# Splitting five block products of the last two projections once more, with their weight sums made ahead on VectorE

## The chip, the cores and the metric

The kernel runs on one core of a Trainium2 chip. The metric is the device time of one execution in microseconds (us), as the median of several runs. Engines are named as the profile names them: PE is TensorE's matmul, PEld its weight load, DVE is VectorE, ACT is ScalarE, POOL is GpSimd, SP is SyncE, which issues most of the transfers here. Each engine works through its own instructions in program order.

## The reference

A cross-attention block in float32: 4 batches of 512 rows, width 512, 16 heads, 512 context rows. The part that the change touches is the MLP at the end.

```python
x = layer_norm(hidden_states, ln1_w, ln1_b)
...
attn = jax.nn.softmax(scores, axis=-1)
out = jnp.einsum('bhqk,bhkd->bhqd', attn, v)
...
out = out @ cproj_w + cproj_b
hidden = out + residual
residual = hidden
y = layer_norm(hidden, ln2_w, ln2_b)
y = jax.nn.gelu(y @ fc_w + fc_b, approximate=True)
y = y @ proj_w + proj_b
return residual + y
```

`fc_w` is 512 x 2048 and `proj_w` 2048 x 512. Everything is float32.

## The kernel before

**Two stages.** The first is attention for all batches, with the MLP of batch 0 and half of that of batch 1 worked in between. The order of instructions is written out by hand. The second stage, `last_mlps` (L590), holds the rest: the second half of batch 1 (`SPLIT` is 1), then batch 2, then batch 3, one after the other. For each batch it runs fc for pairs of 128-wide chunks of the inner dimension (four pairs for batch 1, eight for batches 2 and 3), then proj.

**Seven products instead of eight.** Both matrix products use the Strassen-Winograd scheme: a product of 2 x 2 blocks is made from seven block products, of sums of blocks that other engines prepare. For a left matrix A and a right matrix B the sums are s1 to s4 and t1 to t4, and the products are q1 to q7. `a_sums` (L457) makes s1 to s4 with one add and three subtractions, `b_sums` (L463) t1 to t4. Some sums overwrite a block of their input (`b12` becomes t3, `a21` becomes s3).

- fc: `fc_seven` (L483) does seven products for a pair of chunks, each of two matmuls with 256 columns. Its right sums are `y_sums` (L472), made once per batch from the transposed normed rows `yT` into `ys`; its left sums are those of the weights, `sum_wa` (L580), for pair c+1 while pair c is multiplied. Raw weights and sums have two places each in `gt` (`wa`, `ws`). The two gelus of ACT (L513) leave the result in `ga`.
- proj: `project` (L613). The left matrix is `ga`, its blocks g11 to g22, its sums `gs` from `g_sums` (L603) for two pairs at a time; the right one is the proj weights in `pbt`, their sums in `ptt`, from `p_sums` (L584) for two pairs at a time. Each of the seven products, q1, q2, q3, q6, q7, q5, q4 in this order, is 16 matmuls of 128 x 128 weights and 256 columns for batches 2 and 3 (two row halves t, eight pairs c), and 8 for batch 1. A float32 matmul is two instructions in the profile.

**What stands around the products in `project`.** After q1, `sums()` loads the residual rows of the next batch (`load_hid`, L397), whose bias row GpSimd adds (L357, four adds of 128 x 512); in batch 2 it also made the weight sums `p_sums` for four pairs. After q2, `turns()` transposes the next batch's normed rows on PE (`ln_turn`, L154). Each product's result is joined into the residual rows: VectorE reads PSUM (`join(nc.vector, ...)`, and the adds into `u2p` and `u3p`), GpSimd adds what lies in SBUF (`p1p`, `u2p`, `u3p`). After q5, `middle()` makes the next batch's `y_sums` and `sum_wa(0)` on VectorE; the next batch's fc starts with two products that need neither and a third that needs both. PSUM has four banks of `acc` and four of `half`.

**Batch 3's layernorm.** `cproj` (L382) adds the attention output to rows that lie in the first half of `pbt`, and SP stores them to `xa`. In batch 1's proj, `load_xn` brings them back; during batch 2's fc, VectorE makes their statistics (`stat2`, L406: one bn_stats and one bn_aggr per 128 rows), GpSimd the reciprocal root (`ln_rs`, L131), and VectorE the normed rows (`norm2`, `ln_norm`, L144). `BY_ACT` (L42) lists the norms that ScalarE applies.

**The proj weights of the first four pairs** are loaded during batch 2's fc (L677 to L679), into the part of `pbt` where queries and keys, and then batch 3's rows, lay before.

Of the kernel before, what the change touches and what calls it, by code (L numbers as in the profile page):

```python
# [12 lines left out]
F32 = mybir.dt.float32  # L13
# [7 lines left out]
P = 128  # L21
# [3 lines left out]
NT = L // P  # L25
# [13 lines left out]
IN_XE = (25, 27, 29, 31)  # L39

AT = {u: (u - 5) // 2 for u in (5, 7, 9, 11, 13, 15, 17, 19, 53, 55, 57, 59, 61, 63)}
BY_ACT = ((1, 1), (1, 2))  # L42
MW = 8
WARM = 9
PW = 2 * NT * HG * HD
# [7 lines left out]
def xattn_block(ctx: ExitStack, tc: tile.TileContext, x, encT, mask, q_w, k_w, v_w, c_w, fc_w, p_w, vecs, rows, out):  # L53
# [77 lines left out]
    def ln_rs(key):  # L131

        ve = small.tile([P, NT], F32, tag="ve", name=f"ve{key[0]}_{key[1]}")
        nc.gpsimd.tensor_scalar(ve, S["mv", key][:, :, 1], EPS, 1.0, ALU.add, ALU.mult)
        rs = small.tile([P, NT], F32, tag="rs", name=f"rs{key[0]}_{key[1]}")
        nc.gpsimd.tensor_tensor(rs, ve, nhalf, ALU.pow)
        S["rs", key] = rs
        if key in BY_ACT:
            nm = small.tile([P, NT], F32, tag="nm", name=f"nm{key[0]}_{key[1]}")
            nc.gpsimd.tensor_tensor(nm, S["mv", key][:, :, 0], rs, ALU.mult)  # L140
            nc.gpsimd.tensor_scalar(nm, nm, -1.0, 0.0, ALU.mult, ALU.add)
            S["nm", key] = nm
# [11 lines left out]
    def ln_turn(key, d, xn, dst):  # L154

        w, bi = (LN1W, LN1B) if key[0] == 1 else (LN2W, LN2B)
        tp = acc_tile(f"tp{key[0]}_{key[1]}_{d}")
        for t in range(NT):
            nc.tensor.transpose(tp[:, ts(t, P)], xn[t][:, ts(d, P)], ident)
        wd, bd = vec[:, w + d : w + d + 1], vec[:, bi + d : bi + d + 1]  # L160
        if d in (1, 2) and key not in BY_ACT:
            nc.vector.tensor_scalar(dst[:, d, :], tp, wd, bd, ALU.mult, ALU.add)
        else:
            nc.scalar.activation(dst[:, d, :], tp, AF.Identity, bias=bd, scale=wd)
# [241 lines left out]
    def stat2(b, t):  # L406
        ln_stat((2, b), t, S["h", b, t])
# [46 lines left out]
    def add(engine, o, x0, x1):  # L454
        engine.tensor_tensor(o, x0, x1, ALU.add)  # L455
# [24 lines left out]
    def acc_half(name):  # L480
        return acc_tile(name).rearrange("p (i l) -> p i l", i=2)
# [94 lines left out]
    def load_wa(c):  # L576
        for i in range(2):
            nc.sync.dma_start(out=wa[c % 2][:, i], in_=fc_w[:, 2 * c + i, :, :])
# [5 lines left out]
    def p_sums(c):  # L584
# [2 lines left out]
        b11, b12, b21, b22 = (pb[:, c, k, j * HL : (j + 1) * HL] for k in range(2) for j in range(2))  # L587
        b_sums(b11, b12, b21, b22, pt[:, 0, c], pt[:, 1, c], b12, pt[:, 2, c])

    def last_mlps():  # L590
        last, = pools(ctx, last=1)
        ps_last = ctx.enter_context(tc.tile_pool(name="ps_last", bufs=4, space=PSUM))
        ga = last.tile([P, NP, 2, L], F32, tag="ga", name="ga")
        gs = last.tile([P, 3, NP, HL], F32, tag="gs", name="gs")
        hl = last.tile([P, NT, D], F32, tag="hl", name="hl")
        for t in range(NT):
            S["hid", SPLIT + 1, t] = hl[:, t]
        p1p, u2p, u3p = (last.tile([P, 2, HL], F32, tag=n, name=n) for n in ("p1p", "u2p", "u3p"))

        def half_tile(name):  # L600
            return ps_last.tile([P, 2, HL], F32, tag="half", name=name)

        def g_sums(c):  # L603
            c = slice(c, c + 2)
            a11, a12, a21, a22 = (ga[:, c, k, j * HL : (j + 1) * HL] for j in range(2) for k in range(2))
            a_sums(a11, a12, a21, a22, gs[:, 0, c], gs[:, 1, c], a21, gs[:, 2, c])

        def fc_pair(b, c, sums):
            sums()
            fc_seven(b, c, ga[:, c], [wa[c % 2][:, i] for i in range(2)],  # L610
                     [ws[c % 2][:, i] for i in range(4)], half_tile)

        def project(b, pairs, sums, turns, middle):  # L613
            g11, g12, g21, g22 = (ga[:, :, k, j * HL : (j + 1) * HL] for j in range(2) for k in range(2))
            b11, b12, b21, b22 = (pb[:, :, k, j * HL : (j + 1) * HL] for k in range(2) for j in range(2))
            t1, t2, t3, t4 = pt[:, 0], pt[:, 1], b12, pt[:, 2]
            s1, s2, s3, s4 = gs[:, 0], gs[:, 1], g21, gs[:, 2]

            def product(o, a, w, ts_=range(2)):
                for t in ts_:  # L620
                    for c in pairs:
                        nc.tensor.matmul(  # L622
                            o[:, t], a[:, c, ts(t, P)], w[:, c], start=(c == pairs[0]), stop=(c == pairs[-1])
                        )

            def hid(i, j, t):
                return S["hid", b, 2 * i + t][:, j * HL : (j + 1) * HL]

            def join(engine, i, j, src):
                for t in range(2):  # L630
                    add(engine, hid(i, j, t), src[:, t], hid(i, j, t))

            def store(i, j):
                for t in range(2):
                    nc.sync.dma_start(out=out[b, ts(2 * i + t, P), j * HL : (j + 1) * HL], in_=hid(i, j, t))

            q1, q2 = (acc_half(f"{n}p_{b}") for n in ("q1", "q2"))
            product(q1, g11, b11)
            nc.scalar.copy(p1p, q1)
            sums()  # L640
            product(q2, g12, b21)
            turns()
            q3 = half_tile(f"q3p_{b}")
            product(q3, s4, b22)
            join(nc.vector, 0, 0, q2)
            join(nc.gpsimd, 0, 0, p1p)
            store(0, 0)
            q6 = acc_half(f"q6p_{b}")
            product(q6, s2, t2)
            add(nc.vector, u2p, q6, p1p)  # L650
            join(nc.vector, 0, 1, q3)
            q7 = half_tile(f"q7p_{b}")
            product(q7, s3, t3)
            add(nc.vector, u3p, q7, u2p)
            for i, j, src in ((0, 1, u2p), (1, 0, u3p), (1, 1, u3p)):
                join(nc.gpsimd, i, j, src)
            q5 = half_tile(f"q5p_{b}")
            product(q5, s1, t1)
            join(nc.vector, 0, 1, q5)
            join(nc.vector, 1, 1, q5)  # L660
            store(0, 1)
            store(1, 1)
            middle()
            q4 = half_tile(f"q4p_{b}"), acc_half(f"q4p_{b}")
            for t in range(2):
                product(q4[t], g22, t4, (t,))
                add(nc.vector, hid(1, 0, t), q4[t][:, t], hid(1, 0, t))
                nc.sync.dma_start(out=out[b, ts(2 + t, P), :HL], in_=hid(1, 0, t))

        y_sums(SPLIT)  # L670

        half = FIRST * FQ // 2
        for b, pairs, new in (
            (SPLIT, range(half, NP), ()), (SPLIT + 1, range(NP), range(half)), (SPLIT + 2, range(NP), ())
        ):
            for c in pairs:
                if c in new:  # L677
                    for i in range(2):
                        nc.sync.dma_start(out=pb[:, c, i, :], in_=p_w[ts(2 * c + i, P), :])  # L679
                fc_pair(b, c, lambda: sum_wa(c + 1) if c + 1 < NP else None)  # L680
                if c + 2 < NP:
                    load_wa(c + 2)
                elif b + 1 < B:
                    load_wa(c + 2 - NP)
                if c % 2 == 0 and c != pairs[0]:
                    g_sums(c - 2)

                if b == B - 2:
                    for t in {0: (0,), 1: (1, 2), 3: (3,)}.get(c, ()):
                        stat2(b + 1, t)  # L690
                    if c == 3:
                        ln_rs((2, b + 1))
                    for t in {4: (0,), 5: (1, 2), 7: (3,)}.get(c, ()):
                        norm2(b + 1, t)
            g_sums(NP - 2)

            def sums(b=b, new=new):
                for c in new[::2]:
                    p_sums(c)
                if b + 1 < B:  # L700
                    load_hid(b + 1, range(NT))

            def turns(b=b):
                if b + 1 < B:
                    run(turns2(b + 1))
                if b == SPLIT:
                    load_xn(B - 1)

            def middle(b=b):
                if b + 1 < B:  # L710
                    y_sums(b + 1)
                    sum_wa(0)

            project(b, pairs, sums, turns, middle)
# [17 lines left out]
    def C(b):  # L732
        return [(CHAIN, lambda t=t: cproj(b, t)) for t in range(NT)]
# [190 lines left out]
    run(mlp)  # L924
    load_wa(first_c + 1)
    sum_wa(first_c)
    c = C(B - 1)
    run(c[:2])
    p_sums(first_c + 2)
    run(c[2:])  # L930
    att.close()
    last_mlps()

# [43 lines left out]
```

## Time and profile before

| | us |
|---|---|
| median of three runs | 802.96 (802.51 to 803.77) |
| the profiled execution | 801.93 |
| its span, first to last instruction | 800.2 |

The granted TensorE clock of the profiled execution is 0.998. Busy time by stretch of `last_mlps` (us):

| stretch | length | PE | DVE | ACT | POOL |
|---|---|---|---|---|---|
| batch 1 fc, 549.6 to 574.3 | 24.70 | 24.25 | 19.20 | 5.14 | 0.00 |
| batch 1 proj, 574.3 to 601.3 | 27.00 | 26.76 | 11.78 | 3.48 | 11.24 |
| batch 2 fc, 601.3 to 649.9 | 48.60 | 48.59 | 43.91 | 11.50 | 1.37 |
| batch 2 proj, 649.9 to 700.2 | 50.30 | 50.30 | 22.85 | 3.48 | 11.48 |
| batch 3 fc, 700.2 to 748.6 | 48.40 | 48.40 | 37.23 | 11.49 | 0.00 |
| batch 3 proj, 748.6 to 797.4 | 48.80 | 48.34 | 8.43 | 1.92 | 5.59 |

A line of the timeline gives the start in us from the span's start, the length in us, the engine, the line of the kernel, the operation, the tile written and those read, the shapes and how many were merged; in square brackets is how long the engine had been idle and what ended that. A line of the chain gives the start, the length and what ran. Matmuls overlap in the pipeline, so a single one's listed length is longer than its step to the next.

### The profile page before, as it was taken

Reading aid. Unit: us, or ns where it says so; the run is one execution under the profiler, and the core shown is the slowest. Engines: PE = TensorE matmul, PEld = TensorE weight load, DVE = VectorE, ACT = ScalarE, POOL = GpSimd, SP = SyncE. Lnnn points to the kernel's source line nnn. Section 1 sums busy time; section 2 is a strip of 40 time slices with the busy share of each in tenths; the row PEclk is TensorE's granted clock in tenths of the full one; section 3 lists DMA queues with packets and bytes.
Section 4 is the critical chain, followed back from the end, with each engine's and each line's share of the span. In section 5 each row is a group of like instructions: output and inputs, shape, how many; then the busy total and the mean of one; then the engine's idle time right before and its main releaser. Section 6 shows DMA issues by size and latency. Waiting matters only on the chain.

```text
span 800.2 us, 12085 instructions
## 1 busy us (share of the span) xinstructions
PE 785.3 (98%) x4178; PEld 499.4 (62%) x4178; DVE 573.8 (72%) x1179; ACT 339.5 (42%) x745; POOL 123.9 (15%) x146
## 2 busy tenths in 40 slices
PE   9999999989999999999999999999999999999998
PEld 6545455456655645556553433446888888888887
DVE  3789998888888857779878988546738983368511
ACT  2567765547763636456554479500201220022100
POOL 1210030055121141001220100020040020200011
PEclk9999999999999999999999999999999999999999
DMA  8889999847897777787777799882325330033001
GB/s 325 289 230 241 235 237 244 231 115 182 209 240 196 211 210 192 179 198 199 181 173 213 205 261 246 202 254 93 117 84 172 118 106 14 27 86 86 1 14 40
DMA packets 60957, 137.15 MB, mean 171 GB/s; under 512 B 12464, under 2 KB 15664, under 8 KB 60768
## 3 DMA queue, kind: packets, MB, share of 16 engines
q1 hardware_dynamic: 59472, 132.43, 61.3%
q0 software_dynamic: 896, 2.82, 1.1%
q10 hardware_dynamic: 528, 1.14, 0.7%
q8 instruction: 33, 0.54, 0.3%
q14 instruction: 28, 0.23, 0.1%
HBM read 58.22 MB, written 6.82 MB: 81 GB/s over the span
## 4 chain that ended last, share of the span: by engine, by line
PE 87%; DVE 6%; SPq 3%; ACT 1%; issue 1%; DMA 1%; POOL 0%; DVEq 0%; POOLq 0%; ACTq 0%
PE q L495 20%; PE accp L554 8%; PE sc L262 7%; PE accc L386 7%; PE av L345 7%; PE accv L240 6%; PE acck L218 6%; PE accq L228 5%; PE accf L536 3%; DVE ptt L266 3%; SPq L328 2%; PE q4p L622 2%; PE q3p L622 2%; PE q5p L622 2%; PE q6p L622 2%; PE q7p L622 2%
## 5 line engine op out<-in xcount | busy, mean ns | idle before, releaser
L270 ACT ACTIVATE ptt<-ptt,mn 128x512 f32<-128x512 f32 x256 | 181.7, 711 | 135.1 <-DVE mn L266 134.8
L266 DVE CUSTOM_DVE_ANT_0 ptt<-sc,mb 128x512 f32<-128x512 f32 x256 | 161.0, 685 | 32.7 <-PE sc L262 32.4
L285 DVE STREAM_TRANSPOSE tb<-ptt 128x1024 f32<-128x1024 f32 x96 | 119.2, 1242 | 14.4 <-ACT ptt L270 12.9
L554 PE MATMUL accp<-pbt,gt 128*128 128x512 f32 x192 | 86.7, 600 | 0.0
L495 PE MATMUL q<-yT,gt 128*128 128x256 f32 x320 | 78.9, 379 | 0.0
L262 PE MATMUL sc<-pbt 32*128 32x512 f32 x512 | 73.0, 640 | 4.7 <-DVE mn L266 2.5
L513 ACT ACTIVATE ga<-ga,vec 128x512 f32<-128x512 f32 x40 | 26.7, 714 | 93.2 <-DVE ga L455 93.2
L495 PEld LDWEIGHTS q<-yT,gt 128*128 128x128 f32 x320 | 60.8, 190 | 8.7 <-issue 0.5
L554 PEld LDWEIGHTS accp<-pbt,gt 128*128 128x128 f32 x192 | 35.2, 190 | 49.0 <-issue 46.4
L240 PEld LDWEIGHTS accv<-ptt,xe 128*128 128x128 f32 x512 | 58.7, 192 | 9.5 <-issue 6.7
L495 PE MATMUL q<-ys,gt 128*128 128x256 f32 x240 | 61.8, 380 | 0.5 <-DVE ys L452 0.5
L240 PE MATMUL accv<-ptt,xe 128*128 128x128 f32 x512 | 60.8, 277 | 0.0
L218 PE MATMUL acck<-xe,ptt 128*128 128x512 f32 x128 | 59.1, 605 | 0.0
L228 PE MATMUL accq<-xe,ptt 128*128 128x512 f32 x128 | 58.4, 599 | 0.0
L386 PE MATMUL accc<-wc,oT 128*128 128x512 f32 x128 | 56.6, 596 | 0.0
L495 PEld LDWEIGHTS q<-ys,gt 128*128 128x128 f32 x240 | 45.4, 190 | 7.4 <-DVE ys L452 0.9
L345 PE MATMUL av<-pT,v 128*32 128x256 f32 x768 | 48.1, 392 | 1.8 <-DMA gt<-tb 0.7
L498 ACT COPY p<-q 128x256 f32<-128x256 f32 x28 | 9.9, 355 | 92.5 <-PE q L495 92.5
L270 ACT ACTIVATION_READ_ACCUMULATOR ptt<-ptt,mn 128x1 f32 x256 | 47.8, 187 | 0.0
L252 POOL TENSOR_TENSOR v<-v,row 128x512 f32<-128x512 f32 x16 | 20.4, 1275 | 172.9 <-ACT v L245 172.8
L228 PEld LDWEIGHTS accq<-xe,ptt 128*128 128x128 f32 x128 | 23.6, 190 | 32.4 <-issue 30.4
L262 PEld LDWEIGHTS sc<-pbt 32*128 32x128 f32 x512 | 20.0, 182 | 37.9 <-issue 21.4
(137 smaller groups left out, 1071.4 us busy)
## 6 DMA issues: line engine op xcount, KB each, us to landing
pT<-tb SPq DMA_DIRECT2D x384, 136.0 KB, 2.4
pbt<-p_w_dram SPq DMA_DIRECT2D x40, 256.0 KB, 3.1
gt<-fc_w_dram SPq DMA_DIRECT2D x40, 256.0 KB, 2.6
gt<-tb SPq DMA_DIRECT2D x64, 136.0 KB, 3.4
xe<-tb SPq DMA_DIRECT2D x56, 136.0 KB, 3.1
pbt<-fc_w_dram SPq DMA_DIRECT2D x24, 256.0 KB, 3.9
ptt<-k_w_dram SPq DMA_DIRECT2D x16, 256.0 KB, 3.8
xe<-encT_dram SPq DMA_DIRECT2D x16, 256.0 KB, 4.6
```

The lines of the kernel that those rows point to most:

```text
L218: nc.tensor.matmul(acc, S["wk", w][:, d, :], eT[:, d, :], start=(d == 0), stop=(d == ND - 1))
L228: nc.tensor.matmul(acc, S["wq", w][:, d, :], xT[:, d, :], start=(d == 0), stop=(d == ND - 1))
L240: nc.tensor.matmul(acc[:, ts(t, P)], eT[:, d, ts(t, P)], S["wv", w][:, d, :], start=(d == 0), stop=(d == ND - 1),)
L262: nc.tensor.matmul(sc[:, h, :], qT[r, ts(qt, P)], kT[r, :], start=True, stop=True)
L266: nc.vector.tensor_tensor_reduce(out=s, in0=sc[:, h, :], in1=S["mb", w // NG], scale=1.0, scalar=FMAX, op0=ALU.add, op1=ALU.min, accum_out=mn,
L270: nc.scalar.activation(s, s, AF.Exp, bias=mn, scale=-1.0, accum_out=sums[:, qt, h : h + 1])
L285: nc.vector.transpose(*two_heads[k])
L345: nc.tensor.matmul(av[ts(h, HD), : 2 * P].rearrange(shape, **kw), v[:, t, ts(h, HD)], p[t][h], start=(t == 0), stop=(t == NT - 1),)
L386: nc.tensor.matmul(acc, S["oT", b][:, g, ts(t, P)], wc[:, g, :], start=(g == 0), stop=(g == NG - 1))
L495: nc.tensor.matmul(o, x[:, k], y[:, k], start=(k == 0), stop=(k == 1))
L554: nc.tensor.matmul(acc, gT[q % 2][:, k, ts(t, P)], S["pw", b, q * FQ + k], start=(k == 0), stop=(k == FQ - 1))
L622: nc.tensor.matmul(o[:, t], a[:, c, ts(t, P)], w[:, c], start=(c == pairs[0]), stop=(c == pairs[-1]))
```

## The change

In `project` of batches 2 and 3, the products q2, q3, q6, q7 and q5 are each split in 2 x 2 blocks again and made from seven products (`forty_nine`): four matmuls of 128 columns each, accumulated over four pairs. q1 and q4 stay as they were, and so does the projection of batch 1. `x_sums` makes the left sums of a split product, three on VectorE and one on GpSimd, each 128 x 512 (four pairs of 128), into storage that the product before has left free; `w_sums` makes the right sums, four subtractions of 128 x 512 on VectorE, once for both batches: two of them in batch 1's proj, three between the pairs of batch 2's fc. The seven parts are joined in SBUF by four VectorE adds and one ScalarE copy, so what `join` adds later comes from SBUF.

Batch 3's statistics are made right after cproj, before `last_mlps`, and its norm is applied by ScalarE. The proj weights of pairs 2 and 3 are loaded before cproj, those of pairs 0 and 1 during batch 1's fc; their `p_sums` move from batch 2's proj to batch 1's fc (pairs 2 and 3) and proj (pairs 0 and 1).

```diff
-BY_ACT = ((1, 1), (1, 2))
+BY_ACT = ((1, 1), (1, 2), (2, 3))
...
-        if d in (1, 2) and key not in BY_ACT:
+        if d in (1, 2) and key not in BY_ACT[:2]:
...
+    def load_p(c):
+        for i in range(2):
+            nc.sync.dma_start(out=pb[:, c, i, :], in_=p_w[ts(2 * c + i, P), :])
...
+        p1s = last.tile([P, 2, P], F32, tag="p1s", name="p1s")
+        tt = last.tile([P, 4, 3, NP // 2, P], F32, tag="tt", name="tt")
+        w_more = wsum.rearrange("p a s k f -> p (a s k) f")
+        x_more = [
+            gt[:, n : n + NP // 2 * P].rearrange("p (c n) -> p c n", c=NP // 2) for n in (1024, 1536, 3072)
+        ]
+        def more(i):
+            return [w_more[:, 4 * n : 4 * n + 4] if i == 4 else tt[:, i, n] for n in range(3)]
+        def quarters(m):
+            return [m[:, i * NP // 2 : (i + 1) * NP // 2, ts(j, P)] for i in range(2) for j in range(2)]
+        def w_sums(i, w):
+            w11, w12, w21, w22 = quarters(w)
+            t1, t2, t4 = more(i)
+            sub(t1, w12, w11)
+            sub(t2, w22, t1)
+            sub(w12, w22, w12)
+            sub(t4, w21, t2)
+        def x_sums(x, free):
+            x11, x21, x12, x22 = quarters(x)
+            s1, s2, s4 = free if isinstance(free, list) else quarters(free)[:3]
+            add(nc.vector, s1, x21, x22)
+            sub(s2, s1, x11)
+            sub(x21, x11, x21)
+            sub(s4, x12, s2, nc.gpsimd)
+        def forty_nine(b, name, o, x, w, free, i):
...
+            def product(r, x, w):
+                for c in range(NP // 2):
+                    nc.tensor.matmul(r, x[:, c], w[:, c], start=(c == 0), stop=(c == NP // 2 - 1))
+            product(r1[:, 0], x11, w11)
+            nc.scalar.copy(p1, r1[:, 0])
+            product(r26[:, 0], x12, w21)
+            product(r26[:, 1], s2, t2)
+            add(nc.vector, o[:, 0:4:3], r26[:, :2], p1[:, None, :].broadcast_to([P, 2, P]))
+            product(r57[:, 1], s3, t3)
+            product(r57[:, 0], s1, t1)
+            add(nc.vector, o[:, 1:3], r57[:, :2], o[:, 3:4].broadcast_to([P, 2, P]))
+            add(nc.vector, o[:, 3], r57[:, 0], o[:, 2])
+            product(r34[:, 0], s4, w22)
+            product(r34[:, 1], x22, t4)
+            add(nc.vector, o[:, 1:3], r34[:, :2], o[:, 1:3])
...
             sums()
...
+            if b > SPLIT:
+                x_sums(g12, x_more)
+                x_sums(s4, g11)
+                forty_nine(b, "2", u3p, g12, b21, x_more, 4)
+                turns()
+                join(nc.gpsimd, 0, 0, p1p)
+                join(nc.gpsimd, 0, 0, u3p)
+                store(0, 0)
+                x_sums(s2, g12)
+                forty_nine(b, "3", u3p, s4, b22, g11, 0)
+                join(nc.gpsimd, 0, 1, u3p)
+                x_sums(s3, s4)
+                forty_nine(b, "6", u2p, s2, t2, g12, 1)
+                add(nc.vector, u2p, u2p, p1p)
+                x_sums(s1, s2)
+                forty_nine(b, "7", u3p, s3, t3, s4, 2)
+                add(nc.vector, u3p, u3p, u2p)
+                for i, j, src in ((0, 1, u2p), (1, 0, u3p), (1, 1, u3p)):
+                    join(nc.gpsimd, i, j, src)
+                forty_nine(b, "5", p1p, s1, t1, s2, 3)
+                join(nc.vector, 0, 1, p1p)
+                join(nc.vector, 1, 1, p1p)
+            else:
...
+                w_sums(4, b21)
+                q7 = half_tile(f"q7p_{b}")
...
+                w_sums(0, b22)
+                q5 = half_tile(f"q5p_{b}")
...
-            (SPLIT, range(half, NP), ()), (SPLIT + 1, range(NP), range(half)), (SPLIT + 2, range(NP), ())
+            (SPLIT, range(half, NP), range(half)), (SPLIT + 1, range(NP), ()), (SPLIT + 2, range(NP), ())
...
-                if c in new:
-                    for i in range(2):
-                        nc.sync.dma_start(out=pb[:, c, i, :], in_=p_w[ts(2 * c + i, P), :])
+                if b == SPLIT + 1 and c in (1, 3, 5):
+                    w_sums(c // 2 + 1, (pt[:, 1], pb[:, :, 0, HL:], pt[:, 0])[c // 2])
                 fc_pair(b, c, lambda: sum_wa(c + 1) if c + 1 < NP else None)
...
+                if c - half in new[:-2]:
+                    load_p(c - half)
...
+                if b == SPLIT and c == pairs[1]:
+                    p_sums(new[-2])
                 if b == B - 2:
-                    for t in {0: (0,), 1: (1, 2), 3: (3,)}.get(c, ()):
-                        stat2(b + 1, t)
-                    if c == 3:
-                        ln_rs((2, b + 1))
                     for t in {4: (0,), 5: (1, 2), 7: (3,)}.get(c, ()):
                         norm2(b + 1, t)
...
-                for c in new[::2]:
+                for c in new[:-2:2]:
                     p_sums(c)
...
     sum_wa(first_c)
+    load_p(first_c - 2)
+    load_p(first_c - 1)
     c = C(B - 1)
     run(c[:2])
     p_sums(first_c + 2)
     run(c[2:])
+    for t in range(NT):
+        stat2(B - 1, t)
+    ln_rs((2, B - 1))
     att.close()
     last_mlps()
```

More of the change, by code (lines that the diff above doesn't have):

```diff
@@ new lines, in forty_nine @@
+        def forty_nine(b, name, o, x, w, free, i):
+            x11, s3, x12, x22 = quarters(x)
+            s1, s2, s4 = free if isinstance(free, list) else quarters(free)[:3]
+            w11, t3, w21, w22 = quarters(w)
+            t1, t2, t4 = more(i)
+            r1, r26 = (acc_tile(f"{n}{name}_{b}").rearrange("p (i n) -> p i n", i=4) for n in ("r1", "r26"))
+            r57, r34 = (
+                ps_last.tile([P, 4, P], F32, tag="half", name=f"{n}{name}_{b}") for n in ("r57", "r34")
+            )
+            o = o.rearrange("p t (j n) -> p (t j) n", j=2)
+            p1 = p1s[:, i % 2]
+            def product(r, x, w):
[13 more added lines that the diff above has]
+            add(nc.vector, o[:, 1:3], r34[:, :2], o[:, 1:3])
@@ L635, in store @@
                     nc.sync.dma_start(out=out[b, ts(2 * i + t, P), j * HL : (j + 1) * HL], in_=hid(i, j, t))
-            q1, q2 = (acc_half(f"{n}p_{b}") for n in ("q1", "q2"))
+            q1 = acc_half(f"q1p_{b}")
             product(q1, g11, b11)
@@ L640, in project @@
             sums()
[L641 to L660, printed above, removed]
+            if b > SPLIT:
[21 more added lines that the diff above has]
+            else:
+                q2 = acc_half(f"q2p_{b}")
+                product(q2, g12, b21)
+                turns()
+                q3 = half_tile(f"q3p_{b}")
+                product(q3, s4, b22)
+                join(nc.vector, 0, 0, q2)
+                join(nc.gpsimd, 0, 0, p1p)
+                store(0, 0)
+                q6 = acc_half(f"q6p_{b}")
+                product(q6, s2, t2)
+                add(nc.vector, u2p, q6, p1p)
+                join(nc.vector, 0, 1, q3)
+                w_sums(4, b21)
+                q7 = half_tile(f"q7p_{b}")
+                product(q7, s3, t3)
+                add(nc.vector, u3p, q7, u2p)
+                for i, j, src in ((0, 1, u2p), (1, 0, u3p), (1, 1, u3p)):
+                    join(nc.gpsimd, i, j, src)
+                w_sums(0, b22)
+                q5 = half_tile(f"q5p_{b}")
+                product(q5, s1, t1)
+                join(nc.vector, 0, 1, q5)
+                join(nc.vector, 1, 1, q5)
```

## The prediction

> **What bounds the kernel now.** I read the page first: the busy times, then the chain of work that ended last.
>
> ```profile
> PE 785.3 (98%) x4178; PEld 499.4 (62%) x4178; DVE 573.8 (72%) x1179; ACT 339.5 (42%) x745; POOL 123.9 (15%) x146
> ```
>
> PE holds 87% of that chain, so time is won only by shorter PE work, and lost wherever PE waits. PEclk is 9 in all forty slices: a wait isn't repaid by a better clock. Everything from about 549.6 us on is `last_mlps`. Its chain, in order of time, is nearly unbroken PE; the list of who waited for whom there has PE waiting 0.5 us for the y sums and 0.2 us for a gelu, no more. A whole block product and a group of narrower matmuls (the v projections, moving operand 128 wide) read:
>
> ```profile
> 672.62 6.91 PE q6p L622 x32
> ```
>
> ```profile
> 40.25 3.57 PE accv L240 x32
> ```
>
> Each fp32 matmul is two instructions here: 16 matmuls, 32 instructions, 6.91 us, so 216 ns for 256 columns; and 3.57/32 = 111.6 ns for 128 columns, with a new weight tile each time, as the split products have it.
>
> Then the timeline at the places where VectorE gets new work. First the start of the stage:
>
> ```profile
> 549.61 1.89 PE L495 MATMUL q<-yT,gt 128*128 128x256 f32 x8
> ...
> 549.88 0.69 DVE L387 TENSOR_TENSOR pbt<-accc,pbt 128x512 f32<-128x512 f32 x1 [2.74 <-PE accc L386]
> 550.49 0.68 DVE L452 TENSOR_TENSOR ys<-yT 128x512 f32<-128x512 f32 x1
> ...
> 551.95 1.13 PE L495 MATMUL q<-ys,gt 128*128 128x256 f32 x4 [0.45 <-DVE ys L452]
> ```
>
> VectorE goes from the last cproj add straight to `y_sums`, and PE already waits 0.45 us for it. Next, the end of batch 1:
>
> ```profile
> 595.22 2.77 POOL L455 TENSOR_TENSOR hid<-u3p,hid 128x256 f32<-128x256 f32 x4 [1.64 <-DVE u3p L455]
> ...
> 597.97 0.76 DVE L455 TENSOR_TENSOR h<-q5p,h 128x256 f32<-128x256 f32 x2 [2.83 <-PE q5p L622]
> ...
> 599.31 0.68 DVE L452 TENSOR_TENSOR ys<-yT 128x512 f32<-128x512 f32 x1
> ...
> 603.05 0.73 PEld L495 LDWEIGHTS q<-ys,gt 128*128 128x128 f32 x4 [0.41 <-DVE gt L452]
> ```
>
> The weight load for batch 2's third product waits for VectorE, and the chain puts the matmul at the same 603.05, without a gap: the slack is nil. Third, batch 2's proj, where GpSimd adds the bias row:
>
> ```profile
> 653.35 1.27 POOL L357 TENSOR_TENSOR hid<-hid,row 128x512 f32<-128x512 f32 x1 [23.58 <-DMA hid<-xa]
> 653.41 1.76 DVE L452 TENSOR_TENSOR gs<-gs,ga 128x512 f32<-128x512 f32 x1
> 655.08 4.62 POOL L357 TENSOR_TENSOR hid<-hid,row 128x512 f32<-128x512 f32 x3 [0.47 <-DMA hid<-xa]
> 655.20 1.70 DVE L452 TENSOR_TENSOR gs<-ga,gs 128x512 f32<-128x512 f32 x1
> ```
>
> The same VectorE subtraction takes 0.69 us alone and 1.70 to 1.76 beside a GpSimd add: four in a row (to 658.62 + 1.64 = 660.26), one per GpSimd add. Adds with an operand in PSUM aren't touched: the q3 adds at 592.0 took 0.37 each while GpSimd ran. The Trainium skill (SBUF — State Buffer, Who interferes with whom) says that a VectorE instruction with two SBUF inputs and a GpSimd instruction reading SBUF exclude each other; by it a blocked op would cost 1.27 + 0.69 = 1.96 us (an estimate), the rows say up to 1.76.
>
> **The change, part by part.**
>
> Split products. A product becomes 7 x 4 = 28 matmuls of 128 columns, 56 instructions x 111.6 ns = 6.25 us in place of 6.91: 0.66 saved, ten times: **-6.6 us**. Bounds: v groups that follow the 32-row score matmuls take 3.77 per 32 (0.31 saved, -3.1 in all); transposes of the same width 0.87 per 8 (6.09 a product, -8.2). I take the group without a switch of rows, since none happens here. One rule speaks against it: TensorE: Matmul & The Clock Gate, Back-to-back issue gap, gives 81 ns per matmul at 128 columns and 131 at 512 in streams with weight loads; a line through both gives 98 at 256, so a split product would take 56 x 81 against 32 x 98, 45% more, and ten of them some 31 us more (estimates). This trace has 111.6 against 216, nearly half, and it decides.
>
> (A) The four `stat2` of batch 3 now stand between the last cproj add and `y_sums(1)`. Four in a row earlier in the trace start 0.79 apart:
>
> ```profile
> 159.61 0.65 DVE L128 BATCH_NORM_STATS2 st<-h 128x6 f32<-128x512 f32 x1
> 160.29 0.18 DVE L129 BATCH_NORM_AGGREGATE mv<-st 128x2 f32<-128x6 f32 x1
> 160.39 0.66 DVE L128 BATCH_NORM_STATS2 st<-h 128x6 f32<-128x512 f32 x1
> ```
>
> 4 x 0.79 = 3.2 us, and the `y_sums` behind them are already late: PE's wait grows from 0.45 to 3.6, **+3.2**. The `ln_rs` on GpSimd (1.2 us) hardly blocks: sums beside it at 628.6 took 0.42 as elsewhere. Removing stats (4 x 0.79) and norms (4 x 0.54) from VectorE in batch 2 earns nothing there by itself, for PE didn't wait.
>
> (B) End of batch 1's proj: two `w_sums`, four 512-wide subtractions each; the like in `p_sums` takes 2.53 (660.78 to 663.31, stepped), so 5.06. VectorE was idle 2.03 before u3p and 2.83 before the q5 adds, 4.86 together: without blocking, `y_sums` starts 0.2 late. But `w_sums(4)` meets GpSimd's two joins of u2p, and `w_sums(0)` starts with its four of u3p (0.72 each). Taking turns as in the rows above, one join under way and one between cost the first 1.1 us, three of the four turns cost the second 2.1: 0.2 + 1.1 + 2.1 = **+3.4**, all of it at 603.05, since the q5 adds, `y_sums(2)` and `sum_wa(0)` queue behind it and PE waits for the last. Low bound 0.2 (no blocking), high 4.5 (all six joins in full, 4.3).
>
> (C) Batch 2's fc: three `w_sums` between pairs. Batch 3's timeline shows VectorE back to back there: `g_sums` 719.14 to 721.80 (2.66, each second pair), the next weight sums to 723.26 (1.46), the first add to 724.05 (0.79), the three other adds 1.86: 4.11 per pair without `g_sums`. Two pairs: 8.22 + 2.66 + 2.6 = 13.5, against 2 x 6.045 = 12.1 of PE. PE needs the s2 of the next weights 6.05 + 1.73 = 7.8 after a pair's end; VectorE delivers it at 4.6 now, at 7.2 with one `w_sums`, at 8.6 after the second round: **+0.8** (0 to 1.5), and VectorE is still 1.2 behind when proj begins.
>
> (D) Batch 2's proj. The second product's third part needs s2 of `x_sums(g12)`, which follows `g_sums(6)` on VectorE while GpSimd does four row adds. PE is there after q1 (6.91) and two narrow quarters (1.79): 656.85 + 1.79 = 658.64. On the old schedule s2 would be the sixth VectorE operation from 652.07, at 660.26: 1.6 late. With (C)'s 1.2 of lag only the first of the six is done (653.9) when the row adds begin, the next four meet one each, and s2 is the last: 653.9 + 4 x 1.7 + 0.65 = 661.4, **+2.7**. GpSimd's own part of the x sums (s4, 1.27) queues behind the row adds too, but PE wants it two narrow quarters (1.8) after s2. Low 0 (no blocking: 652.07 + 6 x 0.65 = 656), high 3.5. Batch 3 has no row adds: its s2 is ready at 754.8, needed at 757.3, no wait.
>
> Rest, at nothing. Later `x_sums`, the adds of the parts, ScalarE's copies and four norms of 0.80: a product's sums have the 6.25 us of the product before as cover, ScalarE is busy 11.5 of 48.6 us in batch 2's fc. (The 128-wide add and copy aren't shown; between 0.18 and 0.42, off the path.) The eight weight loads: four issues of 0.45 go on SP between 537.4 and the first xa store at 540.3, where SP is free, the others behind loads of wa; `p_sums(2)` falls in VectorE's gap of 1.96 before 565.3. `p_sums(0)` of batch 1 meets GpSimd's row adds: 580.5 + 4 x 1.7 = 587.3 at worst, the two turn evictions behind it (1.53) end at 588.8; VectorE is idle there from 585.2 to 591.07, so nothing on PE waits but q6 (587.34) for a bank, up to 1.5 us if that cover fails, 0 if GpSimd ends by 585 as I take it.
>
> **Sum:** -6.6 + 3.2 + 3.4 + 0.8 + 2.7 = **+3.5 us**. The profiled execution took 801.93 (span 800.2): 805.4. The median of the runs lies 1.03 above it, 802.96 + 3.5 = **806.5 us**.
>
> **Rivals.**
>
> 1. Faster: the blocking hardly lands on these sums, as GpSimd's joins find gaps. Then B is 0.2, D 0: -6.6 + 3.2 + 0.2 + 0.8 = -2.4, 800.6 us. For: VectorE was busy only 22.9 of 50.3 us in batch 2's proj and turns, so the engines can drift apart. Against: the four blocked rows, and that joins and sums are released by the same events (the end of u2p, of u3p, of a gelu). It decides once B and D together stay under 1.0 us: then the sum is below -1.6. Chance 0.2.
> 2. No change: half of B (1.7) and D without lag (1.6), C at 0: -0.1, 802.9. Chance 0.1.
> 3. Slower still: VectorE becomes the bound inside the split projections. Per batch it has 5 x 1.93 (`x_sums`) + 5 x 1.5 (part adds) + 2.8 = 20 us in 31.3 of PE; GpSimd has 5 x 1.27 + 12 x 0.72 = 15. If all of that blocks, 35 against 31.3: +3.7 a batch, +7.4, 813.9. It decides when over three quarters of GpSimd's time meets such sums. For: the strict turns; against: a full product of cover. Chance 0.1.
> 4. The narrow matmuls step at 3.77 per 32: +3.4 more, 809.9. Chance 0.05.
>
> **How the numbers follow.** The forecast has 0.55. Two thousandths of the time, 1.6 us, is what can be told from no change. Slower 0.55 + 0.1 + 0.05 = 0.7, same 0.1, faster 0.2. Range: at the low end A alone with small B, C, D (rival 1's 800.6 nearly), at the top B and D high with C at 1.5: -6.6 + 3.2 + 4.5 + 1.5 + 3.5 = +6.1, 809.1, and a little of rival 4: 801 to 809.5. The forecast's own is 804.6 to 809.1.
>
> **What would show it.** Split products as chain pieces of 6.2 to 6.3 us; a PE wait of 3.6 us for ys near 552; waits for `sum_wa(0)`'s gt (3.4) at the first pair of batch 2, for gt again (0.8) at its pair 6, for the x sums in gt (2.7) in its second product; none in batch 3. PE unbroken at B and D would make me wrong.

## The result, and the profile after

The median is 809.96 us (806.95 to 811.80, seven runs) against 803.45 us (802.51 to 805.57, seven runs beside them): 1.0074 of the time before, 95% interval 1.0053 to 1.0095. The change made the kernel slower: by 6.5 us between the medians, by 6 by that ratio (of the means), where +3.5 was forecast. The profiled execution took 809.96 us, its span is 808.2 us against 800.2: 8.0 more to account for.

The page of the changed kernel, busy times and the chain by engine:

```profile
PE 781.8 (97%) x4418; PEld 503.5 (62%) x4418; DVE 624.5 (77%) x1257; ACT 345.0 (43%) x759; POOL 152.9 (19%) x166
...
PE 72%; DVE 13%; SPq 7%; DMA 3%; issue 2%; ACT 2%; POOL 0%; DVEq 0%; POOLq 0%; ACTq 0%
```

PE is busy for less time than before (785.3), yet its share of the chain that ended last fell from 87% to 72%, and VectorE's rose from 6% to 13%. Who PE waited for in the last stage, in all, how often, and the longest:

```profile
PE q L495 <- DVE ys L452: 3.6, 1, 3.6
PE q L495 <- DVE gt L452: 3.2, 2, 2.3
PE r L647 <- DVE gt L452: 1.8, 1, 1.8
PE q1p L684 <- ACT ga L513: 1.7, 2, 1.3
```

Before, this list had 0.5 and 0.2 us. Now the last stage by its parts, from the first matmul of each to the first of the next. The columns are the stretch, its length, then busy time and count for PE, PEld, DVE, ACT and POOL, the granted clock, and the DMA share and rate:

```profile
549.42:580.27 30.85, 27.22 (x113) 23.16 (x112) 24.43 (x48) 5.15 (x10) 2.55 (x4) 0.89 0.31 103
580.27:607.01 26.74, 26.41 (x129) 22.89 (x128) 22.24 (x29) 3.48 (x5) 14.59 (x12) 1.00 0.29 99
607.01:660.76 53.75, 50.57 (x225) 43.58 (x224) 46.51 (x91) 13.59 (x25) 0.00 (x0) 0.97 0.29 89
660.76:711.21 50.45, 47.36 (x361) 45.16 (x360) 36.93 (x62) 5.54 (x12) 23.37 (x21) 1.00 0.13 43
711.21:759.56 48.35, 48.35 (x226) 42.56 (x225) 37.23 (x72) 11.51 (x22) 0.00 (x0) 1.00 0.24 72
759.56:804.80 45.24, 45.24 (x345) 43.24 (x343) 26.51 (x47) 3.25 (x8) 18.02 (x17) 1.00 0.06 21
```

| part | before | after | change | what it holds |
|---|---|---|---|---|
| up to the last stage | 549.61 | 549.42 | -0.2 | |
| batch 1 fc | 24.89 | 30.85 | +6.0 | wait for ys 3.6 in place of 0.5; clock 2.8 |
| batch 1 proj | 26.66 | 26.74 | +0.1 | |
| batch 2 fc | 48.62 | 53.75 | +5.1 | waits for gt 2.3 and 0.9; clock 1.7 |
| batch 2 proj | 50.31 | 50.45 | +0.1 | split products -3.3; waits 1.3 (gelu) and 1.8 (x sums) |
| batch 3 fc | 48.34 | 48.35 | 0.0 | |
| batch 3 proj | 48.51 | 45.24 | -3.3 | split products, no wait |
| after PE's last | 3.3 | 3.4 | +0.1 | |

The rows marked "clock" are the surprise. Two parts have a mean clock under 1.00, and inside them the granted clock is exactly half for one stretch each. The first begins in the last 1.2 us of the longest wait (it ends at 554.94), the second 0.6 us behind the next longest (it ends at 611.22):

```profile
553.78:560.61 6.83, 5.67 (x13) 4.54 (x14) 4.45 (x10) 0.00 (x0) 2.45 (x4) 0.50 0.00 0
...
611.81:615.22 3.41, 3.41 (x10) 2.71 (x9) 2.51 (x7) 0.00 (x0) 0.00 (x0) 0.50 0.48 154
```

Of the first stretch PE worked 5.67 us at half speed and lost half of that, 2.8; of the second, 1.7. Together 4.5 us that the length of the waits doesn't hold.

### The profile page after: what moved, and what is told of

Same layout as the page of the kernel before. It is cut to its first block, busy times and chain, and to the rows that moved or that the text cites. A ratio compares the mean times of both kernels' runs of the same rounds, so it can differ in the third digit from the quotient of the medians.

```text
span 808.2 us, 12737 instructions
## 1 busy us (share of the span) xinstructions
PE 781.8 (97%) x4418; PEld 503.5 (62%) x4418; DVE 624.5 (77%) x1257; ACT 345.0 (43%) x759; POOL 152.9 (19%) x166
## 4 chain that ended last, share of the span: by engine, by line
PE 72%; DVE 13%; SPq 7%; DMA 3%; issue 2%; ACT 2%; POOL 0%; DVEq 0%; POOLq 0%; ACTq 0%
PE q L495 15%; PE r L647 8%; PE accp L554 7%; SPq L328 7%; PE sc L262 6%; PE av L345 6%; PE acck L218 6%; PE accv L240 6%; PE accc L386 5%; PE accq L228 5%; PE accf L536 3%; DVE ptt L266 2%; DVE ga L455 2%; PE q4p L684 2%; DMA pT<-tb 2%
## 5 line engine op out<-in xcount | busy, mean ns | idle before, releaser
L495 PE MATMUL q<-yT,gt 128*128 128x256 f32 x320 | 80.8, 386 | 0.0
L495 PE MATMUL q<-ys,gt 128*128 128x256 f32 x240 | 64.6, 393 | 6.8 <-DVE ys L452 3.6
L345 PE MATMUL av<-pT,v 128*32 128x256 f32 x768 | 46.4, 382 | 3.7 <-DMA ptt<-v_w_dram 1.6
L455 DVE TENSOR_TENSOR ga<-q,ga 128x512 f32<-128x512 f32 (+1 forms) x60 | 36.2, 603 | 11.4 <-PE q L495 7.4
L386 PEld LDWEIGHTS accc<-wc,oT 128*128 128x128 f32 x128 | 23.8, 190 | 31.5 <-issue 29.8
```

The lines of the kernel that those rows point to most:

```text
L345: nc.tensor.matmul(av[ts(h, HD), : 2 * P].rearrange(shape, **kw), v[:, t, ts(h, HD)], p[t][h], start=(t == 0), stop=(t == NT - 1),)
L386: nc.tensor.matmul(acc, S["oT", b][:, g, ts(t, P)], wc[:, g, :], start=(g == 0), stop=(g == NG - 1))
L495: nc.tensor.matmul(o, x[:, k], y[:, k], start=(k == 0), stop=(k == 1))
```

## The experiments

The part of the program up to the last stage, which none of the edits below touches in its PE work, ends between 548.8 and 552.6 us from one profiled execution to the next, with or without a half-clock stretch of its own near 173 us. So parts of the last stage are compared, and times only where several runs give an interval. Three of the kernels ran once: without the joins 804.03 us, with the sums at other pairs 812.15, with the x sums first 806.26.

### The statistics behind the y sums

```diff
+    y_sums(SPLIT)
     c = C(B - 1)
...
-        y_sums(SPLIT)
```

> The changed kernel with y_sums(1) moved ahead of the last cproj adds, so that the four stat2 follow it; nothing else differs. Both theories expect PE's wait of 3.6 us for ys at the start of the last stage to go. Theory 1 (a long PE wait is followed by a stretch at half the clock): the half-clock stretch of 6.8 us after it goes too, so batch 1's fc falls from 30.85 us to 24.4, by 6.4 (3.6 + 2.8), and the span from 808.2 to about 802. Theory 2 (the clock falls by itself, the wait costs its length alone): a half-clock stretch remains somewhere, batch 1's fc or the span falls by 3.6 only, to about 804.6.

Batch 1's fc of that kernel, as a stretch:

```profile
551.96:576.13 24.17, 24.17 (x113) 21.28 (x112) 21.98 (x44) 5.14 (x10) 1.76 (x4) 1.00 0.40 131
```

24.17 us, 6.7 less: wait and half clock went together, and even the 0.45 us that the kernel before waited. Length alone would have left 27.2. The time: 805.61 us median, 1.0018 of the kernel before (0.9999 to 1.0038).

### The sums of batch 1's proj, moved, and without the joins

```diff
+                w_sums(4, b21)
+                w_sums(0, b22)
                 q6 = acc_half(f"q6p_{b}")
...
-                w_sums(4, b21)
...
-                w_sums(0, b22)
```

> The changed kernel with both w_sums of batch 1's proj moved ahead of the add into u2p, where VectorE has nothing to do for some 3 us and the joins of u2p and u3p are not yet released. Theory 1 (VectorE's late sums, made later by GpSimd's joins, and the half clock after the wait): the wait of 2.3 us at the start of batch 2 falls below 0.3, the half-clock stretch of 3.4 us behind it goes, batch 2's fc falls from 53.75 us by 4.0 to about 49.7. Theory 2 (the wait comes from the amount of VectorE work, wherever it stands): the wait stays over 1.5 us.

The wait fell from 2.3 to 0.46 us, no half clock followed, and batch 2's fc took 50.17 us, 3.6 less. The bound of 0.3 for the wait was missed by little; the amount of work as the cause is out. 806.54 us median, 1.0039 (1.0020 to 1.0057).

The second edit leaves `w_sums` where the change put them and takes out batch 1's `join(nc.gpsimd, ...)` of u2p and u3p, so these terms are missing from its output; it serves for timing alone:

```diff
-                for i, j, src in ((0, 1, u2p), (1, 0, u3p), (1, 1, u3p)):
-                    join(nc.gpsimd, i, j, src)
                 w_sums(0, b22)
```

> The changed kernel without batch 1's six GpSimd joins of u2p and u3p (three quarters of batch 1's rows 0 to 511 miss those terms). Blocking theory (two SBUF inputs against a GpSimd add): the eight subtractions of w_sums(4) and w_sums(0), 0.68 to 1.21 us each now, take 0.68 each; y_sums(2) starts about 3 us sooner, and the wait at the start of batch 2 falls from 2.3 us to 0.0 to 0.3. If the subtractions are slow for another reason (their strided quarters, the tiles they write), they stay at up to 1.2 us and the wait stays over 1.5 us.

The timeline at `w_sums(0)`, first the changed kernel, with GpSimd's joins beside it, then this one:

```profile
602.32 4.51 POOL L455 TENSOR_TENSOR hid<-u3p,hid 128x256 f32<-128x256 f32 x4 [2.44 <-DVE u3p L455]
602.87 1.10 DVE L452 TENSOR_TENSOR tt<-pbt,tt 128x512 f32<-128x512 f32 x1
603.89 1.21 DVE L452 TENSOR_TENSOR pbt<-pbt 128x512 f32<-128x512 f32 x1
605.03 1.21 DVE L452 TENSOR_TENSOR tt<-pbt,tt 128x512 f32<-128x512 f32 x1
```

```profile
600.00 0.69 DVE L452 TENSOR_TENSOR tt<-pbt,tt 128x512 f32<-128x512 f32 x1
600.61 0.68 DVE L452 TENSOR_TENSOR pbt<-pbt 128x512 f32<-128x512 f32 x1
601.21 0.68 DVE L452 TENSOR_TENSOR tt<-pbt,tt 128x512 f32<-128x512 f32 x1
```

Same line, same tiles: 0.7 us without GpSimd's adds beside them, 1.1 to 1.2 with them. The wait at the start of batch 2 is gone from the list, and so is the half clock behind it. The sums are slow because GpSimd's adds run beside them, not for their strides or tiles.

### The sums of batch 2's fc at other pairs

```diff
-                if b == SPLIT + 1 and c in (1, 3, 5):
-                    w_sums(c // 2 + 1, (pt[:, 1], pb[:, :, 0, HL:], pt[:, 0])[c // 2])
+                if b == SPLIT + 1 and c in (1, 2, 3):
+                    w_sums(c, (pt[:, 1], pb[:, :, 0, HL:], pt[:, 0])[c - 1])
```

> The changed kernel with the three w_sums of batch 2's fc ahead of pairs 1, 2 and 3 in place of 1, 3 and 5. Theory 1 (VectorE falls behind by 1.4 us for each two pairs that have both g_sums and w_sums): with one of the three where no g_sums stands, the wait of 0.9 us at pair 6 goes, VectorE is level at the end of fc, and PE's wait of 1.3 us for the last gelu in q1 goes; together 2.2 to 2.5 us, batch 2's fc 52.8 us at most. The wait for the x sums in the second product stays between 1.0 and 1.8. Theory 2 (the amount of sums in batch 2's fc is what counts, not the place): the waits stay.

Half a miss. The wait in fc fell from 0.9 to 0.4 us and moved to pair 4, the gelu's from 1.3 to 0.4, batch 2's fc took 53.17 us (52.8 at most was expected). But the wait for the x sums grew from 1.8 to 2.5, with half a clock behind it. VectorE's lag was not what set it: it began with `g_sums(6)` 4.2 us after q1's start in place of 5.1, yet s2 came 11.9 us after q1's start here and 12.2 in the changed kernel. The row adds start some 3.7 us after q1's start in both, and hold up four of VectorE's sums here, three there (the first of the row adds was done by then). PE shares out nearly the same wait between gelu and sums: 0.4 + 2.5 here, 1.3 + 1.8 there.

### The x sums ahead of the row adds

```diff
-            sums()
             if b > SPLIT:
                 x_sums(g12, x_more)
                 x_sums(s4, g11)
+            sums()
+            if b > SPLIT:
```

> The changed kernel with the two x_sums of the second product issued ahead of the loads and row adds of the next batch's residual rows, so that GpSimd's part of the first x sums, which waits for VectorE's s2, stands before the four row adds in its queue. Blocking theory: none of g_sums(6) and x_sums(g12) takes over 0.8 us, s2 is ready some 4 us sooner, and PE's wait of 1.8 us in the second product goes; the wait for the gelu (1.3 us) stays; batch 2's proj falls from 50.45 to about 48.7 us. If the wait comes from the number of VectorE sums alone, it stays over 1 us.

VectorE and, below it, GpSimd in that kernel's batch 2 proj:

```profile
666.74 0.69 DVE L455 TENSOR_TENSOR gt<-ga 128x512 f32<-128x512 f32 x1
667.46 0.69 DVE L452 TENSOR_TENSOR gt<-gt,ga 128x512 f32<-128x512 f32 x1
```

```profile
668.32 1.56 POOL L452 TENSOR_TENSOR gt<-ga,gt 128x512 f32<-128x512 f32 x1 [61.68 <-ACT p1p L701]
...
672.92 5.41 POOL L357 TENSOR_TENSOR hid<-hid,row 128x512 f32<-128x512 f32 x4
```

s2 is made by 668.15, 9.2 us after q1's start, and the row adds (L357) come after it. The wait of 1.8 us is gone, batch 2's proj took 48.42 us (48.7 expected). One thing stood out: the wait of 2.3 us at the start of batch 2 was there, but its half clock wasn't.

### All four

> All four places mended: y_sums(1) ahead of the last cproj adds, both w_sums of batch 1 ahead of the add into u2p, those of batch 2's fc ahead of pairs 1, 2 and 4, x_sums ahead of the row adds. Theory 1 (the split products save 6.6 us, and all that was lost are PE's waits and the half clock after the longest): waits of PE in the last stage under 1 us together, no half-clock stretch there, last stage's parts 24.2, 26.7, 48.7, 47.1, 48.35 and 45.2 us, the time 6 to 7.5 us under the kernel before (about 0.992 of it). A rival (the split products' gain is lost in some fixed way, so that no order beats the kernel before): not faster than 0.998.

The edits above together, with `w_sums` ahead of pairs 1, 2 and 4, which takes two of them away from `g_sums`. PE's waits in its last stage, and the chain in batch 3's proj:

```profile
PE q1p L684 <- ACT ga L513: 1.3, 2, 0.8
PE q L495 <- DVE gt L452: 0.4, 1, 0.4
```

```profile
749.15 6.91 PE q1p L684 x32
756.06 31.26 PE r L647 x280
787.33 6.92 PE q4p L684 x32
```

798.00 us median (796.61 to 801.05, six runs) against 804.02 us (17 runs): 0.9932 of the kernel before, 0.9911 to 0.9954. No half clock in the stage; its parts are 24.18, 26.89, 49.05, 47.90, 48.35 and 45.25 us, 5.7 less than before's in sum. The waits are 1.7 us where under 1 was expected, two of them for a gelu. The split products' gain is real, and the order alone had hidden it.

The longest wait left, 0.8 us for the last gelu of batch 2, starts on ScalarE, whose norms of batch 3 are part of the change:

```profile
646.09 1.50 ACT L146 ACTIVATE hn<-hn,nm,rs 128x512 f32<-128x512 f32 x2
647.50 0.35 ACT L498 COPY p<-q 128x256 f32<-128x256 f32 x1
647.88 0.69 DVE L455 TENSOR_TENSOR ga<-q,p 128x512 f32<-128x512 f32 x1 [1.60 <-ACT p L498]
```

Two norms stand ahead of the copy that VectorE's next add needs, and VectorE is idle for 1.60 us; the chain runs through both norms, that add and the last gelu to q1. All eleven profiles with the change have this idle time of 1.60 us, the one before has none of over 1 us there. No run moves the norms, so what this costs in time is not shown.

### One wait, of four lengths

```diff
+    for t in range(N):
+        stat2(B - 1, t)
+    y_sums(SPLIT)
+    for t in range(N, NT):
+        stat2(B - 1, t)
```

in the kernel with all four mended, for N of 4, 2, 1 and 3.

> As four_moved, but y_sums(1) again behind all four stat2: one PE wait of 3.6 us in a stage that has otherwise none. Theory 1: the wait of 3.6 us, and a half-clock stretch of 3.4 or 6.8 us behind it, in batch 1's fc, which goes from 24.2 to between 29.4 and 30.9 us; so the wait costs 5 to 7 us in all. Waits alone: 27.7 us and no half clock.

> As four_moved, but two of the four stat2 ahead of y_sums(1): a PE wait of 0.45 + 2 x 0.79 = 2.0 us. So far waits of 1.8 us left the clock as it was, and those of 2.3 and more halved it. Theory 1 with a limit between: batch 1's fc 24.2 + 2.0 = 26.2 us, or 27.9 where the half clock comes; waits alone: 26.2.

> As four_moved, but one of the four stat2 ahead of y_sums(1): a PE wait of 0.45 + 0.79 = 1.2 us. Rule read from the ten profiles so far (the stretches of the profile laid out in steps of 3.41 us: a step with 2.04 us or more of idle PE is followed by half the clock, one with 1.81 or less is not): no half clock whatever the phase, batch 1's fc 24.2 + 1.2 = 25.4 us. If any wait in this place halves the clock: 27.1.

> As four_moved, but three of the four stat2 ahead of y_sums(1): a PE wait of 0.45 + 3 x 0.79 = 2.8 us. By the rule it depends on the phase: with over 2.04 of the 2.8 us in one step, half the clock for 3.4 us and batch 1's fc 24.2 + 2.8 + 1.7 = 28.7 us; parted more evenly between two steps, no half clock and 27.0. If the wait's length alone decides (2.0 and more always), half clock in either phase.

| N | PE's wait for ys | half clock with it | batch 1 fc | median |
|---|---|---|---|---|
| 0 (all four mended) | 0 | none | 24.18 | 798.00 |
| 1 | 1.2 | none | 25.69 | one run, 800.88 |
| 2 | 2.0 | 3.41 | 28.17 | one run, 801.82 |
| 3 | 2.8 | 3.41 | 28.96 | one run, 800.00 |
| 4 | 3.6 | 3.41 | 29.53 | 804.26 (ten runs) |

The runs of N = 1, 2 and 3 are single ones, so their times say nothing about each other; the parts do. The half clock of N = 2 as a stretch:

```profile
556.60:560.01 3.41, 3.41 (x10) 2.66 (x9) 3.31 (x9) 0.00 (x0) 1.58 (x4) 0.50 0.00 0
```

With N = 4 the kernel is at 1.0005 of the one before (0.9989 to 1.0020): one wait of 3.6 us, with its half clock, ate the whole gain, 6.3 us between the medians (5.4 in batch 1's fc of the profiles). N = 1 gave 25.69 where 25.4 was expected; the other 0.3 us stays open.

**When the clock halves.** The stretches start at whole steps of 3.41 us from each other: 611.81 - 553.78 = 17 x 3.413. I laid all twelve profiles out in such steps, from each one's own half-clock starts, and summed PE's idle time in each. At full clock every step with 2.04 us or more of it (2.04 to 3.4, 22 of them) is followed by half the clock; none with 1.8 or less is. The ends of the programs, where PE's work runs out within a step, fit: 2.05, 2.17 and 3.36 us of idle time there were followed by half the clock, 1.98 wasn't. A step at half the clock is followed by a second one where PE idled 0.60 us or more in it (0.60 to 1.16, four of them), by the full clock at 0.51 or less. These are limits read from the profiles; no run varied where the steps lie. They explain the odd run: there the 2.33 us fell on two steps, 1.7 and some 0.6. PE's timeline of the kernel with x sums first:

```profile
611.04 1.13 PE L495 MATMUL q<-ys,gt 128*128 128x256 f32 x4 [2.33 <-DVE gt L452]
```

And the step that holds most of this wait, as a stretch:

```profile
607.00:610.40 3.40, 1.71 (x8) 1.15 (x7) 3.29 (x8) 0.37 (x1) 0.00 (x0) 1.00 0.46 154
```

PE is idle for 1.69 us of 3.40 there, and the clock holds at 1.00 behind it. The Trainium skill (TensorE: Matmul & The Clock Gate, What's actually happening) describes such a free-running window of some 3.4 us; it puts the fall to half after an idle window. These runs agree on the window and differ on the rest: 2.0 us of idle time in one were enough.

## Why the prediction was right, and where its size was off

The direction held, for the reason given: PE had almost no slack, VectorE's new sums and GpSimd's blocking made it wait, and the waits together outweighed the saving. The size did not: 809.96 us lies above the forecast of 806.5 and the range's end of 809.5; measured by the kernel before it is 802.96 x 1.0074 = 808.9. By its steps:

- **Split products, -6.6.** Measured 31.26 us for 280 instructions, 111.6 ns each: 6.25 a product, -3.3 a batch, as forecast; the rival with 3.77 per 32 is out.
- **(A), +3.2.** The wait went from 0.45 to 3.6. The size held as a wait.
- **(B), +3.4.** Measured 2.3. Place and mechanism held (gone without the joins); the size was too large because a sum beside a 128 x 256 GpSimd add took 1.10 to 1.21 us, so a turn cost 0.4 to 0.5 (five of them, 2.3 in all), where I had added each join's 0.7 in full.
- **(C), +0.8.** Measured 0.9 at pair 6.
- **(D), +2.7.** Measured 1.8, and 1.3 more that I hadn't booked: VectorE is late with the last gelu's input, and q1 itself waits for it. I charged the lag to the x sums alone; by the run with other pairs the lag hardly moves s2, which the row adds set. The two waits make 3.1 for 2.7. (The rows behind the price of a blocked sum read 1.64 to 1.76, not 1.70 to 1.76.)
- **ScalarE's norms, put at nothing** because ScalarE is busy 11.5 of 48.6 us in batch 2's fc. That is a mean; two of them stand ahead of a copy that VectorE needs and make it idle for 1.60 us, on the way to the wait of 1.3. A copy without norms ahead made it idle for 0.20 at 641.31, so by these rows the norms are some 1.4 us of VectorE's lateness (an estimate).
- **Batch 3 without a wait, GpSimd's `ln_rs`, the moved loads and `p_sums`:** nothing in the trace says otherwise. VectorE as the bound inside the split products (rival 3) is out: after the first sums of batch 2, the chain holds 25.01 us of their PE work without a gap.

**The step that failed is above all the sentence that dismissed the clock:** "PEclk is 9 in all forty slices: a wait isn't repaid by a better clock". True, but a wait can be charged for by a worse one, and I never asked. The sum of waits was foreseen as 10.1 and came to some 9.6, near it partly by luck, since (B) was priced 1.1 too high and (D) 0.4 too low. What the sum lacks is the 4.5 us of half clock at two of the waits: -6.6 + 9.6 + 4.5 = 7.5 of the 8.0 us by which the span grew; the last 0.5 stays open. It could have been seen in the profile before. A slice there is 20 us wide, and a stretch of 3.4 us at half leaves a digit of 9. Its PE timeline in the attention part has this line:

```profile
172.68 0.66 PE L159 MATMUL tp<-ident,xn 128*128 128x128 f32 x4 [3.05 <-ACT pbt L231]
```

The stretch behind that wait reads:

```profile
173.44:176.85 3.41, 3.41 (x32) 1.38 (x32) 2.30 (x4) 0.72 (x1) 1.66 (x1) 0.50 0.00 0
```

A PE wait of 3.05 us, and 0.8 us behind it 3.41 us at half the clock, 1.7 lost. With that row, the two waits that were foreseen as longer, (A) and (B), cost 1.7 more each, and the forecast is 3.5 + 3.4 = +6.9.

## What to carry to other kernels

A PE wait had a second price here: where it took some 2 us or more of a 3.4 us step, the matmuls of the next step or two ran at half speed, so the wait of 2.3 us cost 4.0 and that of 3.6 cost 5.4 to 6.7. When work is added to an engine that is off the critical path, look for the few points where PE waits for the end of that engine's queue, and put new work behind them, not ahead: here four such moves, each a line or two, turned 1.007 into 0.993. Keep sums with two SBUF operands on VectorE away from adds that GpSimd is given at the same moment, and count the row adds, not only the sums. On an engine that is mostly idle, ask what a new instruction stands ahead of: the two norms on ScalarE came before a copy that VectorE waited for.

## What the runs showed of the hardware

- The granted clock halved only at steps of 3.41 us, and from full speed only after a step with 2.04 us or more without PE work (22 of 22); up to 1.98 us in one step it never did. Once halved it stayed so for a second step where PE idled 0.60 us or more in the first (4 of 4), not at 0.51 or less. Of the waits of 2.3 us in one place, one of four was spared by where the steps lay. The wait of 3.05 us in the attention part was spared in the same way in the changed kernel (1.5 and 1.6 in two steps).
- Matmuls with a 128-wide moving operand and a new weight tile each stepped at 111.6 ns for 280 in a row, 0.517 of the 216 ns at 256 columns.
- VectorE sums of 128 x 512 with both operands in SBUF: 0.68 alone, mostly 1.10 to 1.21 beside GpSimd adds of 128 x 256 and 1.64 to 1.77 beside those of 128 x 512 (less where the two only met at an end). Adds from PSUM took 0.42 at 128 x 256 in either case.
